# A mixture-of-experts layer on one core: 39 tiles of 256 rows become 25 of 256 and 21 of 128, and the inner columns are cut into chunks of 128

## The chip, the cores and the metric

The kernel runs on one core of a Trainium2 chip. A core has a matrix engine (TensorE, PE in the profile; its weight loads are listed as PEld), a vector engine (DVE), a scalar engine (ACT), a general engine (POOL), an engine that mostly issues transfers (SyncE, SP; SPq are its issues) and 16 DMA engines. Each engine runs its own instructions in order and waits for others by semaphores. The metric is the time of one execution on the device, in microseconds (us).

## What is computed

A transformer block in float32: attention with a residual, then a mixture of experts with a residual. Layernorm stands before and after each half.

```python
x = x + layernorm(attention(layernorm(x)))     # x: (4, 1024, 256), 16 heads of 16, rotary positions
x = x + layernorm(moe(layernorm(x)))

def moe(x):                                     # T = 4096 tokens, D = 256, E = 8 experts, H = 684, K = 2
    d2 = sum(x * x) + sum(cen * cen) - 2 * x @ cen.T
    w, sel = top_k(sqrt(max(d2, 1e-12)), K)     # two experts for each token
    w = softmax(w)
    we = zeros(T, E); we[t, sel] += w
    out = 0
    for e in range(E):
        h = silu(x @ Wg[e] + bg[e]) * (x @ W1[e] + b1[e])    # (T, 684)
        out = out + we[:, e:e + 1] * (h @ W2[e] + b2[e])
    return out
```

The biases bg, b1 and b2 are drawn at random, not zero.

## The kernel before

**Attention.** It takes the first 60% of the span. Its work is cut into steps: a step handles 128 keys against 512 queries for four heads, with scores on TensorE (L671, L678: tiles sc), exp on ACT, the weighted sum on TensorE (L740: av), and for the maxima of steps to come another set of score matmuls (L590: pm) that DVE reduces (L594: part). Between them come works of other kinds: splitting and stacking of heads (L531: ps), values, the output projection (`finish`), layernorm and routing (`settle`). A planner written into the kernel orders all this. A `Work` is a generator that yields before each piece the costs it expects ("P500 D400" means 500 ns of TensorE, then 400 of DVE); works are sorted by due step, and the planner runs the first whose costs fit into the model it keeps of when each engine will be free. The model knows nothing of transfers. TensorE, DVE and ACT execute in the order that the planner emits.

`late_constants` (L191) is such a work, with due step 40: the squares of the centroids, their sum, and the output bias turned through the output projection (pbo, L209). It is issued as soon as it fits.

**Transfers at the start, on SP in program order.** Loads of x and of the attention weights; the wg load of expert 0; then `rows<-empty` (L226), which clears the DRAM tile `rows` (34816 rows: each expert has a region of 4096, since any routing must fit, and 2048 lie behind them) in 34 DMAs of 1 MB; then the building of `wall` (L233 to L248), a DRAM tile that holds for each expert one block of 128 partitions: gate weights, inner weights, output weights in six chunks of 114 rows, and the biases. Per expert these are four DMAs (wg and w1: 128 x 2 x 684, w2: 114 x 6 x 256, b2: one row), and two at the end for bg and b1, all from DRAM to DRAM. Each DMA on SP takes one of eight semaphore lanes in turn, and its issue waits until the DMA that used the lane before has landed; so at most eight are under way.

**Routing.** `settle` finds for each token its two experts and the place in their regions, and scatters the normalized token with its weight and target id to `rows` (L929, on POOL, eight scatters for each 512 tokens). The number of rows per expert is known only at run time.

**Experts.** After attention a small table on DVE (L1038 to L1069) gives each of MT = 39 tiles its expert and its first row: 8192 rows in tiles of 256 are 32, and 7 more cover the incomplete last tiles of the experts, whatever the routing. For each tile j:

- `fetch` (L1076): SP reads the two table entries, loads 256 rows (xt) and the block of the expert's weights (w, a 128-partition part, a 114-partition part and one row; L1085, L1089). Weights are loaded anew for each tile, three buffers deep.
- `transposed` (L1095): four transposes on TensorE (px), one copy on DVE (xT).
- `up` (L1106): for each of six chunks of 114 inner columns four matmuls of 256 columns (two halves of the 256 input channels, gate and inner), Silu on ACT (sil), bias and product on DVE (h).
- `down` (L1127): for each half of the tile's rows six matmuls over the chunks (pe), the 115th row of the last chunk being a row of ones against b2; then the token's weight on DVE (yo) and a scatter on POOL (L1146).

The loop (L1189 on) is written out by hand for SP, TensorE, DVE and ACT: two chunks of up of tile j, half of down of tile j-1, two chunks, the other half, fetch of tile j+2, transposes of tile j+1, two chunks. Then the results of each token's two rows are added, normalized and stored.

A float32 matmul leaves two records in the trace ("x32" is sixteen matmuls).

Of the kernel before, what the change touches and what calls it, by code (L numbers as in the profile page):

```python
# [8 lines left out]
F32 = mybir.dt.float32  # L9
# [7 lines left out]
P = 128  # L17
# [14 lines left out]

TS = 256
NTS = TS // P
MT = 2 * B * T // TS + NE - 1
XW = C + 2
CAP = B * T
NROW = NE * CAP + NE * TS
NRES = 2 * B * T + MT * TS
O1, O2, OG, WW = KC * FF, 2 * KC * FF, 2 * KC * FF + NF * C, 2 * KC * FF + NF * C + 2 * NF  # L40
# [3 lines left out]
def sandwich(  # L44
# [168 lines left out]


# [18 lines left out]
    wall = tc.dram_tile([NE, P, WW], F32, name="wall")  # L233
    for e in range(NE):
        for i, w in enumerate((wg, w1)):
            nc.sync.dma_start(
                out=wall[e, :, i * O1 : (i + 1) * O1].rearrange("p (k f) -> p k f", k=KC),
                in_=w[e].rearrange("(k p) f -> p k f", p=P),
            )
        nc.sync.dma_start(  # L240
            out=wall[e, :FP, O2:OG].rearrange("p (f c) -> p f c", f=NF),
            in_=w2[e].rearrange("(f p) c -> p f c", p=FP),
        )
        nc.sync.dma_start(out=wall[e, FP : FP + 1, OG - C : OG], in_=b2[e : e + 1, :])
    for i, bias in enumerate((bg, b1)):
        nc.sync.dma_start(
            out=wall[:, :FP, OG + i * NF : OG + (i + 1) * NF].rearrange("e p f -> p e f"), in_=bias
        )  # L248
# [353 lines left out]
    def outputs(u, av):  # L602
# [32 lines left out]
        if g == NG - 1:  # L635
            fast = u == len(order) - 1

            before_ = list(settling.values())
            closing[b, qb] = Work(
                finish(b, qb, fast), at_step[0] + 6,  # L640
                after=[back] + [closing[k] for k in closing] + before_[:-1],
            )
            settling[b, qb] = Work(
                settle(b, qb, fast), at_step[0] + 8, after=[closing[b, qb]] + before_
            )
# [346 lines left out]
    with tc.manual_schedule(engines={ET.PE, ET.DVE, ET.Activation}):  # L992
# [17 lines left out]
        Work(late_constants(), 40)  # L1010
# [26 lines left out]

    pc = bank("counts")  # L1038
    nc.tensor.matmul(pc[:, :NE], ones, seen, start=True, stop=True)
    one = slice(0, 1)  # L1040
    cnt = const.tile([1, NE], I32, tag="cnt", name="cnt")
    nc.vector.tensor_scalar(cnt, pc[one, :NE], float(TS - 1), None, ALU.add)
    nc.vector.tensor_scalar(cnt, cnt, TS.bit_length() - 1, None, ALU.arith_shift_right)
    num = const.tile([1, NE], F32, tag="num", name="num")
    nc.vector.tensor_copy(num, cnt)
    tri = const.tile([1, NE, NE], F32, tag="tri", name="tri")
    nc.vector.tensor_tensor(
        tri, num[:, None, :].to_broadcast([1, NE, NE]), before[one], ALU.mult
    )
    first = const.tile([1, NE], F32, tag="first", name="first")  # L1050
    nc.vector.tensor_reduce(first, tri, AX.X, ALU.add)
    sh = [1, MT, NE]
    le = const.tile(sh, F32, tag="le", name="le")
    nc.vector.tensor_tensor(
        le, first[:, None, :].to_broadcast(sh), tiles_at[one, :MT, None].to_broadcast(sh), ALU.is_le
    )
    tab = const.tile([1, 2, MT], F32, tag="tab", name="tab")
    nc.vector.tensor_reduce(tab[:, 0, :], le, AX.X, ALU.add)
    nc.vector.tensor_scalar(tab[:, 0, :], tab[:, 0, :], -1.0, None, ALU.add)
    nc.vector.tensor_tensor(le, le, first[:, None, :].to_broadcast(sh), ALU.mult)  # L1060
    at0 = const.tile([1, MT], F32, tag="at0", name="at0")
    nc.vector.tensor_reduce(at0, le, AX.X, ALU.max)
    nc.vector.tensor_tensor(at0, tiles_at[one, :MT], at0, ALU.subtract)
    nc.vector.tensor_scalar(at0, at0, float(TS), None, ALU.mult)
    nc.vector.scalar_tensor_tensor(
        tab[:, 1, :], tab[:, 0, :], float(CAP), at0, ALU.mult, ALU.add
    )
    tabi = const.tile([1, 2, MT], I32, tag="tabi", name="tabi")
# [3 lines left out]
    hs = [hp.tile([P, NF, TS], F32, tag=f"h{i}", name=f"h{i}") for i in range(2)]  # L1072
    for h in hs:
        nc.gpsimd.memset(h[96:P, NF - 1, :], 1.0)

    def fetch(j):  # L1076
        e = nc.sync.value_load(tabi[:, 0, j : j + 1], min_val=0, max_val=NE - 1)
        r = nc.sync.value_load(tabi[:, 1, j : j + 1], min_val=0, max_val=NROW - TS)
        xt = mp.tile([P, NTS, XW], F32, tag="xt", name=f"xt_{j}")
        nc.sync.dma_start(  # L1080
            out=xt, in_=rows[bass.ds(r, TS), :].rearrange("(i p) c -> p i c", p=P)
        )
        w = wpool.tile([P, WW], F32, tag="w", name=f"w_{j}")
        for rows_, cols in ((P, slice(0, O2)), (FP, slice(O2, WW))):
            nc.sync.dma_start(  # L1085
                out=w[:rows_, cols],
                in_=wall[bass.ds(e, 1), :rows_, cols].rearrange("e p w -> (e p) w"),
            )
        nc.sync.dma_start(  # L1089
            out=w[FP : FP + 1, OG - C : OG],  # L1090
            in_=wall[bass.ds(e, 1), FP : FP + 1, OG - C : OG].rearrange("e p w -> (e p) w"),
        )
        return xt, w

    def transposed(j, xt):  # L1095
        pt = bank(f"px_{j}").rearrange("p (k t) -> p k t", k=KC)
        for i in range(NTS):
            for k in range(KC):
                nc.tensor.transpose(  # L1099
                    pt[:, k, i * P : (i + 1) * P], xt[:, i, k * P : (k + 1) * P], ident  # L1100
                )
        xT = mp.tile([P, KC, TS], F32, tag="xT", name=f"xT_{j}")
        nc.vector.tensor_copy(xT, pt)
        return xT

    def up(j, w, xT, f2):  # L1106

        h = hs[j % 2]
        for f in (2 * f2, 2 * f2 + 1):
            pu = psu.tile([P, 2, TS], F32, tag="pu", name=f"pu_{j}_{f}")  # L1110
            for i in range(2):
                for k in range(KC):
                    c0 = i * O1 + k * FF + f * FP
                    nc.tensor.matmul(  # L1114
                        pu[:FP, i, :], w[:, c0 : c0 + FP], xT[:, k, :],
                        start=(k == 0), stop=(k == KC - 1),
                    )
            sil = sp.tile([FP, TS], F32, tag="sil", name=f"sil_{j}_{f}")
            nc.scalar.activation(  # L1119
                sil, pu[:FP, 0, :], AF.Silu, bias=w[:FP, OG + f : OG + f + 1]  # L1120
            )
            nc.vector.scalar_tensor_tensor(  # L1122
                h[:FP, f, :], pu[:FP, 1, :], w[:FP, OG + NF + f : OG + NF + f + 1], sil,
                ALU.add, ALU.mult,
            )

    def down(j, xt, w, i):  # L1127

        h = hs[j % 2]
        po = bank(f"pe_{j}_{i}")  # L1130
        for f in range(NF):
            n = FP + (f == NF - 1)
            nc.tensor.matmul(  # L1133
                po[:, :C], h[:n, f, i * P : (i + 1) * P], w[:n, O2 + f * C : O2 + (f + 1) * C],
                start=(f == 0), stop=(f == NF - 1),
            )
        y = mp.tile([P, C], F32, tag=f"y{i}", name=f"yo_{j}_{i}")
        ids = mp.tile([P, 1], I32, tag=f"ids{i}", name=f"ids_{j}_{i}")
        own = sp.tile([P, 1], F32, tag=f"own{i}", name=f"own_{j}_{i}")
        at = xt[:, i, C + 1 : C + 2]  # L1140
        nc.vector.tensor_scalar(
            own, at, float(2 * B * T), float(j * TS), ALU.is_ge, ALU.mult
        )
        nc.vector.tensor_tensor(ids, own, at, ALU.add)
        nc.vector.tensor_scalar(y, po[:, :C], xt[:, i, C : C + 1], None, ALU.mult)  # L1145
        sent = nc.gpsimd.indirect_dma_start(  # L1146
            out=res[:, :],
            out_offset=bass.IndirectOffsetOnAxis(ap=ids, axis=0),
            in_=y,
            in_offset=None,  # L1150
        )
        tc.declare_no_dep(sent.ins, group="results", reason="rows of their own")
        tc.add_to_no_dep_group("results", sent.ins)
# [37 lines left out]
    with tc.manual_schedule(engines={ET.SP, ET.PE, ET.DVE, ET.Activation}):  # L1191
        ready, last = [fetch(0), fetch(1)], None
        xT = transposed(0, ready[0][0])
        for j in range(MT):
            xt, w = ready.pop(0)
            up(j, w, xT, 0)
            for i in range(2):
                if last is not None:
                    down(*last, i)
                if i == 1:  # L1200
                    if j + 2 < MT:
                        ready.append(fetch(j + 2))
                    if j + 1 < MT:
                        nxt = transposed(j + 1, ready[0][0])
                up(j, w, xT, i + 1)
            xT, last = nxt, (j, xt, w)
        for i in range(2):
            down(*last, i)
# [86 lines left out]
```

## Time and profile before

| | |
|---|---|
| Time, median of three runs | 1920.45 us (1914.9 to 1924.0) |
| The profiled execution | 1901.81 us, its span 1900.0 us |
| Mean granted TensorE clock | 0.946 |
| TensorE busy | 1699.6 us (89%) |
| DVE, ACT, POOL busy | 1067.6, 880.6, 572.7 us |
| up: matmuls (L1114), ACT (L1119), DVE (L1122) | 422.3, 110.3, 112.9 us busy |
| down: matmuls (L1133) | 214.9 us busy |
| DMA | 101036 packets, 196.99 MB |

The page shows the span in 40 equal slices of 47.5 us; each digit is the busy share of a slice in tenths. "x1872" in a group is its number of records. The granted clock of TensorE by slice is

```profile
PEclk8899999999999999999999995799999999999975
```

and the issues of the transfers that the change touches are listed with their number, size and, for some, the median time from issue to landing:

```profile
w<-wall SPq DMA_DIRECT2D x39, 1368.0 KB, 6.7
rows<-empty SPq DMA_DIRECT2D x34, 1032.0 KB, 15.5
...
wall<-in_w_dram SPq DMA_DIRECT2D x16, 684.0 KB
xt<-rows SPq DMA_DIRECT2D x39, 258.0 KB
wall<-in_wg_dram SPq DMA_DIRECT2D x8, 684.0 KB
```

### The profile page before, as it was taken

The page shows a single profiled execution, that of the slowest core. Times are in us where ns is not written, and L with a number is a line of the kernel's source. Part 1 is how long each engine was busy: PE and PEld are TensorE (multiplying, and loading weights), DVE is VectorE, ACT ScalarE, POOL GpSimd, SP SyncE. Part 2 cuts the span into 40 slices and gives each one's busy share as a digit, 9 for nine tenths or more (in the row PEclk, how much of TensorE's full clock was granted, in tenths as well). Part 3 has the DMA queues.
Part 4 walks back from the last instruction along what each step waited for, and adds up shares of the span by engine and source line. Part 5 has one row for each costly group of instructions (what it writes and reads, how often), then busy time and mean ns, then how long its engine had stood idle before and what let it go on. Part 6 is the DMA issues. An engine that isn't in the chain of part 4 may idle for free. (4 is left out here: it accounts for less than half of the span.)

```text
span 1900.0 us, 27442 instructions
## 1 busy us (share of the span) xinstructions
PE 1699.6 (89%) x9640; PEld 1068.7 (56%) x9640; DVE 1067.6 (56%) x2522; ACT 880.6 (46%) x1766; POOL 572.7 (30%) x1068
## 2 busy tenths in 40 slices
PE   4989999999999999999999992799999999999940
PEld 3444445544444454445444441688888888888840
DVE  6576687686677687676678844133333333333346
ACT  2357676776776676676575671111111111111113
POOL 5652422543471544542432132011111111111104
PEclk8899999999999999999999995799999999999975
DMA  8997500100000001000000001844444444444434
GB/s 251 301 299 207 142 1 12 34 34 12 23 1 23 24 34 34 1 12 23 1 35 18 29 31 36 274 167 163 165 162 163 163 164 167 163 164 166 167 125 155
DMA packets 101036, 196.99 MB, mean 104 GB/s; under 512 B 8094, under 2 KB 80437, under 8 KB 95907
## 3 DMA queue, kind: packets, MB, share of 16 engines
q1 hardware_dynamic: 83410, 160.65, 26.1%
q0 software_dynamic: 9040, 26.21, 4.1%
q10 hardware_dynamic: 8448, 8.39, 1.4%
q8 instruction: 76, 1.25, 0.3%
q14 instruction: 62, 0.50, 0.1%
HBM read 132.22 MB, written 79.86 MB: 112 GB/s over the span
## 5 line engine op out<-in xcount | busy, mean ns | idle before, releaser
L594 DVE TENSOR_REDUCE part<-pm 128x1 f32<-128x512 f32 x1024 | 647.6, 684 | 212.3 <-PE pm L590 209.2
L682 ACT ACTIVATE e<-sc 128x512 f32<-128x512 f32 x1024 | 538.2, 603 | 199.1 <-PE sc L678 191.4
L1114 PE MATMUL pu<-xT,w 128*114 128x256 f32 x1872 | 422.3, 383 | 7.4 <-DMA x<-resid 4.6
L1114 PEld LDWEIGHTS pu<-xT,w 128*114 128x114 f32 x1872 | 334.1, 180 | 77.1 <-issue 5.0
L1119 ACT ACTIVATE sil<-pu,w 114x256 f32<-114x256 f32 x234 | 110.3, 474 | 504.3 <-PE pu L1114 495.4
L1122 DVE SCALAR_TENSOR_TENSOR h<-pu,w,sil 114x256 f32<-114x256 f32 x234 | 112.9, 484 | 337.1 <-ACT sil L1119 337.0
L590 PE MATMUL pm<-stack,stack 64*128 64x512 f32 x960 | 267.9, 472 | 20.3 <-DVE part L594 15.5
L740 PE MATMUL av<-e,v 128*32 128x512 f32 x2048 | 281.7, 622 | 0.0
L1146 POOL DMA_INDIRECT res<-yo,ids x78 | 74.8, 959 | 567.8 <-DVE yo L1145 562.7
L671 PE MATMUL sc<-stack,stack 64*128 64x512 f32 x960 | 238.9, 439 | 1.3 <-ACT oT L766 0.7
L678 PE MATMUL sc<-shift,bring 64*128 64x512 f32 x1024 | 235.3, 407 | 3.7 <-ACT shift L579 3.5
L590 PEld LDWEIGHTS pm<-stack,stack 64*128 64x128 f32 x960 | 120.0, 188 | 200.8 <-DVE part L594 118.2
L1133 PE MATMUL pe<-w,h 114*128 114x256 f32 x936 | 214.9, 379 | 0.0
L1133 PEld LDWEIGHTS pe<-w,h 114*128 114x128 f32 x936 | 178.1, 190 | 25.1
L671 PEld LDWEIGHTS sc<-stack,stack 64*128 64x128 f32 x960 | 114.9, 187 | 64.1 <-issue 23.2
L678 PEld LDWEIGHTS sc<-shift,bring 64*128 64x128 f32 x1024 | 120.6, 190 | 25.8 <-ACT shift L579 14.2
L1145 DVE TENSOR_SCALAR yo<-pe,xt 128x256 f32<-128x256 f32 x78 | 37.7, 483 | 104.4 <-PE pe L1133 104.4
L538 ACT CAST stack<-ps 128x512 fp32r<-128x512 f32 x124 | 73.5, 595 | 49.3 <-PE ps L531 48.9
L531 PEld LDWEIGHTS ps<-ident_r,split 128*128 128x128 f32 x512 | 52.2, 144 | 64.3 <-POOL split L262 22.0
L531 PE MATMUL ps<-ident_r,split 128*128 128x128 f32 x512 | 69.4, 264 | 16.0 <-POOL split L262 15.9
L740 PEld LDWEIGHTS av<-e,v 128*32 128x32 f32 x2048 | 41.2, 109 | 72.6 <-issue 66.3
L929 POOL DMA_INDIRECT rows<-xr,to x64 | 62.7, 980 | 62.3 <-DVE to L924 44.7
(246 smaller groups left out, 1432.6 us busy)
## 6 DMA issues: line engine op xcount, KB each, us to landing
w<-wall SPq DMA_DIRECT2D x39, 1368.0 KB, 6.7
rows<-empty SPq DMA_DIRECT2D x34, 1032.0 KB, 15.5
w<-wall SPq DMA_DIRECT2D x39, 689.3 KB
wall<-in_w_dram SPq DMA_DIRECT2D x16, 684.0 KB
xt<-rows SPq DMA_DIRECT2D x39, 258.0 KB
wall<-in_wg_dram SPq DMA_DIRECT2D x8, 684.0 KB
xb<-in_x_dram POOLq DMA_DIRECT2D x8, 512.0 KB, 4.3
resid<-xb SPq DMA_DIRECT2D x8, 512.0 KB, 3.8
```

Of the source, the lines that this page charges most:

```text
L531: nc.tensor.transpose(ps[:, t * P : (t + 1) * P], splits[b, g, half][:, t, is_k, 2 * pr : 2 * pr + 2].rearrange("p h n d -> p (h n d)"), i ...
L590: nc.tensor.matmul(pm, q[r, t * P : (t + 1) * P], k_[r, half * TB : (half + 1) * TB], start=True, stop=True,)
L594: nc.vector.tensor_reduce(part[:, i, 2 * pr + s, half : half + 1], pm, AX.X, ALU.max)
L671: nc.tensor.matmul(sc, k_[r, kb * P : (kb + 1) * P], q[r, qb * TB : (qb + 1) * TB], start=True, stop=False,)
L678: nc.tensor.matmul(scs[s], bring[pr][r, :], shift[u][r, :], start=False, stop=True)
L682: nc.scalar.activation(e, scs[s], AF.Exp, scale=1.0 / HD**0.5)
L740: nc.tensor.matmul(av[32 * j : 32 * j + 32, :], v_aug[kb][:, 4 * g + j, :], es[j], start=(kb == 0), stop=(kb == NT - 1),)
L1114: nc.tensor.matmul(pu[:FP, i, :], w[:, c0 : c0 + FP], xT[:, k, :], start=(k == 0), stop=(k == KC - 1),)
L1119: nc.scalar.activation(sil, pu[:FP, 0, :], AF.Silu, bias=w[:FP, OG + f : OG + f + 1])
L1122: nc.vector.scalar_tensor_tensor(h[:FP, f, :], pu[:FP, 1, :], w[:FP, OG + NF + f : OG + NF + f + 1], sil, ALU.add, ALU.mult,)
L1133: nc.tensor.matmul(po[:, :C], h[:n, f, i * P : (i + 1) * P], w[:n, O2 + f * C : O2 + (f + 1) * C], start=(f == 0), stop=(f == NF - 1),)
L1146: sent = nc.gpsimd.indirect_dma_start(out=res[:, :], out_offset=bass.IndirectOffsetOnAxis(ap=ids, axis=0), in_=y, in_offset=None,)
```

## The change

**Tiles.** MW = 25 tiles of 256 rows come first: any routing of 8192 rows to eight experts fills at least 25. What each expert has left goes into MH = 21 tiles of 128 rows. 25 x 256 + 21 x 128 = 9088 rows are computed in place of 9984. The table on DVE is made in two parts (`whole_tiles` and `table`, 36 operations for 14). `rows` gets one more clearing DMA (35).

**Chunks.** 684 = 5 x 128 + 44. A chunk of 128 has four matmuls as before. In the remainder, gate and inner share one matmul for each half of the channels: its stationary operand is 44 gate columns followed by the last 64 inner columns, of which w1's last 44 land on partitions 64 to 107. For that wall holds w1's last 64 columns a second time, next to wg. The remainder's h goes to a tile hr: rows 0 to 43 for the tile's first 128 rows, 64 to 107 for the second, each followed by a row of ones for b2. Down issues the remainder's matmuls of both halves first (45 rows each, on different rows of the array), then five chunks for each half.

**Wall and fetch.** Wall is built by eleven DMAs for each expert, 88 in all: wg in two of 128 x 684, w1's last 64 columns in two, its first 640 in two, w2 in one of 128 x 5 x 256, its last 44 rows twice, b2 twice. A fetch is xt, one DMA of 128 x 4068 for all but the remainder of w2, and one of 45 x 256 for each half.

**Biases.** They no longer lie in the layout that wall wants. bg and b1 are loaded to SBUF (`natural`, 114 x 48 each; the load of bg is issued before the clearing of rows, that of b1 after it, by the order in which the tile framework places them on SP); TensorE transposes them (plin), ACT copies them (flat), SP writes them to a DRAM tile (lin) and reads that back as 16 x 684 (lined); TensorE transposes six pieces (pbias_), POOL and ACT fill a tile (biases), and SP writes it to wall. All of this from plin on is in two new pieces of `late_constants`, and `closing`, the work that ends a block of attention, must now come after them.

**Loop.** For each tile: remainder, chunks 0 and 1, first half of down of the tile before, chunks 2 and 3, the rest of down, fetch of j+2, transposes of j+1, chunk 4.

```diff
-MT = 2 * B * T // TS + NE - 1
+MW = -(-(2 * B * T - NE * (TS - 1)) // TS)
+MH = (2 * B * T - MW * TS) // P + NE - 1
+MT = MW + MH
...
@@ late_constants
+        yield "P200 A400"
+        pc = bank("plin", pssc)
+        n = NE * NF
+        for i in range(2):
+            nc.tensor.transpose(pc[:n, i * FP : (i + 1) * FP], natural[:, i, :], ident[:FP, :FP])
+        flat = ap1.tile([n, 2, FP], F32, tag="eq", name="flat")
+        nc.scalar.copy(flat, pc[:n, : 2 * FP].rearrange("p (i f) -> p i f", i=2))
+        for i in range(2):
+            nc.sync.dma_start(
+                out=lin[i].rearrange("e (f p) -> (e f) p", p=FP), in_=flat[:, i, :]
+            )
+        lined = ap1.tile([2 * NE, FF], F32, tag="oT", name="lined")
+        nc.sync.dma_start(out=lined, in_=lin.rearrange("i e f -> (i e) f"))
+        yield "P900 A400"
+        pc = bank("pbias_", pssc).rearrange("p (f i) -> p f i", i=2 * NE)
+        for f in range(NC + 1):
+            m = P if f < NC else FR
+            nc.tensor.transpose(
+                pc[:m, f, :], lined[:, f * P : f * P + m], ident[: 2 * NE, : 2 * NE]
+            )
+        biases = ap1.tile([P, NE, 2, NC + 1], F32, tag="gt", name="biases")
+        pool.memset(biases, 0.0)
...
+        nc.sync.dma_start(
+            out=wall[:, :, OB:OR].rearrange("e p w -> e p w"),
+            in_=biases.rearrange("p e i f -> p e (i f)"),
+        )
...
     wall = tc.dram_tile([NE, P, WW], F32, name="wall")
+    lin = tc.dram_tile([2, NE, FF], F32, name="lin")
+    natural = ap1.tile([FP, 2, NE * NF], F32, tag="gt", name="natural")
+    for i, bias in enumerate((bg, b1)):
+        nc.sync.dma_start(out=natural[:, i, :], in_=bias.rearrange("p e f -> p (e f)"))
     for e in range(NE):
-        for i, w in enumerate((wg, w1)):
-            nc.sync.dma_start(
-                out=wall[e, :, i * O1 : (i + 1) * O1].rearrange("p (k f) -> p k f", k=KC),
-                in_=w[e].rearrange("(k p) f -> p k f", p=P),
-            )
+        for w, to, cols in (
+            (wg, 0, slice(0, FF)), (w1, FF, slice(FF - (P - R2), FF)), (w1, FF + P - R2, slice(0, NC * P))
+        ):
+            n = cols.stop - cols.start
+            for k in range(KC):
+                nc.sync.dma_start(
+                    out=wall[e, :, k * WK + to : k * WK + to + n], in_=w[e, k * P : (k + 1) * P, cols]
+                )
         nc.sync.dma_start(
-            out=wall[e, :FP, O2:OG].rearrange("p (f c) -> p f c", f=NF),
-            in_=w2[e].rearrange("(f p) c -> p f c", p=FP),
-        )
-        nc.sync.dma_start(out=wall[e, FP : FP + 1, OG - C : OG], in_=b2[e : e + 1, :])
+            out=wall[e, :, O2:OB].rearrange("p (f c) -> p f c", f=NC),
+            in_=w2[e, : NC * P].rearrange("(f p) c -> p f c", p=P),
+        )
+        for r in (0, R2):
+            nc.sync.dma_start(out=wall[e, r : r + FR, OR:], in_=w2[e, NC * P :])
+            nc.sync.dma_start(out=wall[e, r + FR : r + FR + 1, OR:], in_=b2[e : e + 1, :])
...
-                after=[back] + [closing[k] for k in closing] + before_[:-1],
+                after=[back, late] + [closing[k] for k in closing] + before_[:-1],
...
-        Work(late_constants(), 40)
+        late = Work(late_constants(), 40)
...
-    def up(j, w, xT, f2):
-
+    def up(j, w, xT, f):
+        n = tiles[j] * P
         h = hs[j % 2]
...
+        pu = psu.tile([P, 2, TS], F32, tag="pu", name=f"pu_{j}_{f}")
+        m = P if f < NC else R2 + FR
+        for i in range(2 if f < NC else 1):
+            for k in range(KC):
+                c0 = k * WK + (i * (FF + P - R2) + f * P)
+                nc.tensor.matmul(
+                    pu[:m, i, :n], w[:, c0 : c0 + m], xT[:, k, :n],
+                    start=(k == 0), stop=(k == KC - 1),
+                )
...
+    def down(j, xt, w):
+
+        pos = [bank(f"pe_{j}_{i}") for i in range(tiles[j])]
+        for i, po in enumerate(pos):
+            r = slice(i * R2, i * R2 + FR + 1)
+            nc.tensor.matmul(po[:, :C], hr[j % 2][r, :], w[r, OR:], start=True, stop=False)
+        for i, po in enumerate(pos):
+            for f in range(NC):
+                nc.tensor.matmul(
+                    po[:, :C], hs[j % 2][:, f, i * P : (i + 1) * P],
+                    w[:, O2 + f * C : O2 + (f + 1) * C], start=False, stop=(f == NC - 1),
+                )
...
-            up(j, w, xT, 0)
...
+            for f in (NC, 0, 1):
+                up(j, w, xT, f)
+            next(last, None)
+            for f in (2, 3):
+                up(j, w, xT, f)
+            for _ in last:
+                pass
+            if j + 2 < MT:
+                ready.append(fetch(j + 2))
+            if j + 1 < MT:
+                nxt = transposed(j + 1, ready[0][0])
+            up(j, w, xT, 4)
+            xT, last = nxt, down(j, xt, w)
+        for _ in last:
+            pass
```

## The prediction

> **What bounds the kernel now.** I read the page first (busy shares and slices), then the chain of waits, then SP's and TensorE's timelines where the diff touches them.
>
> ```profile
> PE 1699.6 (89%) x9640; PEld 1068.7 (56%) x9640; DVE 1067.6 (56%) x2522; ACT 880.6 (46%) x1766; POOL 572.7 (30%) x1068
> PE   4989999999999999999999992799999999999940
> DMA  8997500100000001000000001844444444444434
> ```
>
> TensorE is busy 89% of the span, in tenths 9 through attention (slices 3 to 24) and again in the experts (27 to 37). Whatever TensorE loses in either stage goes to the end, and whatever matrix work falls away in the experts comes off. DMA is loaded in slices 1 to 5, then idle to slice 25.
>
> The chain of waits (start, us, what) in the experts:
>
> ```profile
> 1244.82 6.91 PE pu L1114 x32
> 1251.73 2.59 PE pe L1133 x12
> 1254.32 3.46 PE pu L1114 x16
> 1260.81 6.91 PE pu L1114 x32
> ```
>
> Nothing but TensorE stands there, with a period of 1260.81 - 1244.82 = 15.99 us. One matmul of 256 columns leaves two records, and a record is 6.91/32 = 0.216 us. A tile of 256 rows has 48 records of up (10.37), 24 of down (5.18) and four transposes (0.44 together, from 1260.21 to 1260.65): 15.99. So 39 tiles take 623.4 us.
>
> SP's timeline at the start (start, us, what):
>
> ```profile
> 15.72 0.76 SPq L236 DMA_DIRECT2D wall<-in_wg_dram  x1
> 16.60 117.78 SPq L226 DMA_DIRECT2D rows<-empty  x34
> 134.43 3.37 SPq L236 DMA_DIRECT2D wall<-in_w_dram  x1
> ...
> 145.26 0.83 SPq L236 DMA_DIRECT2D wall<-in_wg_dram  x1
> ...
> 147.86 8.07 SPq L244 DMA_DIRECT2D wall<-in_b_dram  x1
> 155.98 0.64 SPq L236 DMA_DIRECT2D wall<-in_wg_dram  x1
> ```
>
> SP clears the rows for 118 us (3.46 per DMA), then builds wall at 11 us per expert until 228 us. No engine waits for any of it in attention now. TensorE's timeline at that time:
>
> ```profile
> 90.23 1.13 PE L209 MATMUL pbo<-wo,bvs 128*128 128x256 f32 x4
> 91.29 1.07 PE L740 MATMUL av<-e,v 128*32 128x512 f32 x8
> 92.28 0.53 PE L531 MATMUL ps<-ident_r,split 128*128 128x128 f32 x4
> 92.75 0.50 PE L590 MATMUL pm<-stack,stack 64*128 64x512 f32 x2
> 93.08 0.39 PE L671 MATMUL sc<-stack,stack 64*128 64x512 f32 x2
> ```
>
> These five rows are the place where the new bias transposes go.
>
> **Part 1: the biases (a new wait).** The planner runs the late constants early: pbo is at 90.2 us. In the changed kernel's order, TensorE has after pbo four av, four ps, two pm, then the two plin transposes, which wait for both loads of natural; then sc, ps, pm (about 4 us of work), then six pbias_ transposes, which wait for lined. TensorE runs in order, so behind plin stand all scores, and behind them exp on ACT, the maxima on DVE and the rest. POOL's memset of biases waits for plin too, ahead of its splits.
>
> What do the two waits wait for? SP's order is: natural from bg, 35 DMAs of rows, natural from b1, 88 DMAs of wall, two of lin, lined. So lined comes after everything.
> Rows: the last one was issued one step before 134.43; one more DMA (+3.5), one wg load less ahead (a 128x2x684 load moves 256 packets of 2736 B over 16 engines, at 115 ns each in the trace 1.84). The last packets of the rows, at 138.9 to 144.8 by engine, then end near 146.5, and b1 lands at about 148.
> Wall: before, one expert's 11 us are 2 x 1.84 for wg and w1, some 6.5 for w2, whose 114 rows keep only 0.40 of the engines busy (133 GB/s from 166 to 168 us, against 1.04 and 357 GB/s from 162 to 164), and 0.2 per DMA. After: wg 1.84, w1 with the copied block 1.9, w2 of 128 rows 640 packets of 1024 B at 51 ns over 16 engines 2.04, the remainders 0.4: 6.2 us, and 11 DMAs at 0.2 come to 8.4 if nothing overlaps, 6.2 if all does. SP's own issues (0.6 to 0.8 for the large ones, 0.24 for the one-row load at L1089) come to 11 x 0.55 = 6.1. I take 7.7, near the upper one because at most eight DMAs are under way at a time: 62 us for eight experts. A second way: sixteen wo loads of 16 KB took 11.78 us, 0.74 each; 88 x 0.74 = 65. Bounds: 17.4 MB at the best rate of the trace (461 GB/s, 1192 to 1194 us) is 38; the old 11 us is 88.
> Then lin and lined, each issued after the one before has landed, at some 2 us each (a 512 KB store of resid lands after 3.8, of which its 32 packets per engine at 51 ns are 1.6). Lined: 146.5 + 62 + 4 = 212.5.
> TensorE reaches plin at 93.1 and has 4 us of work until lined; it restarts cold (granted clock 0.50 at 1214 to 1216 after an idle time, 1.00 later), 1.5 us once. Lost: 212.5 - 93.1 - 4 + 1.5 = 117, less some 2 that it makes up because DVE is ahead afterwards (all its waits for DVE's sums at L594 to 1150 us are 18 us): **+115, bounds 91 and 141**. The matmuls themselves (8 of at most 128 columns) are under 1 us, ACT's and POOL's copies lie in the idle time. Wall's new end, about 215 instead of 230 us, is a thousand us before its first reader: nothing. Behind lined on SP stand wall's biases and then the first store of resid, which came at 342 us: not reached.
>
> The Trainium skill, "DMA: Bandwidth & Descriptors", "Rules for kernel authors", says that many small transfers should be merged, since under 64 KB one pays mostly overhead; its section on the anatomy of a DMA gives that overhead as about 2 us. It speaks against 88 small DMAs and the detour of lin. Paid one after the other that would be an estimated 176 us for wall, and the time would be some 115 us above mine; the row of sixteen loads at 0.74 shows them overlapping, so I keep the row.
>
> **Part 2: tiles of 256 rows, chunks of 128.** Up goes from 24 to 22 matmuls, down from 12 to 10 and the remainder's pair, which sits on different rows of the array. 44 + 20 records at 0.216 = 13.82, transposes 0.44, the pair 0.43 if its two matmuls run together, 0.86 if not: 14.69 or 15.12. Two score matmuls on 64 rows each took 0.23 us together (806.64 to 806.87 us), so I take 14.69.
>
> **Part 3: tiles of 128 rows.** 44 records of up with 128 columns. No up row of this width exists; the transposes are the nearest: 0.109 per load of 128 columns and its 128-column matmul. The pdist group (96 loads, 11.6 us busy) gives 0.121 as the other end. 44 x 0.109 = 4.80, 12 records of down 2.59, two transposes 0.22: 7.61. Per chunk TensorE takes 0.87 us, ACT and DVE less than their 0.47 and 0.48 at 256 columns: covered. The copy of xT (0.69 at 512 columns) comes late behind DVE's chunk: 0.3. I take 7.9.
> TensorE's page, "TensorE: Matmul & The Clock Gate", "Back-to-back issue gap", gives 81 ns per sustained load and matmul of 128 columns. By it a tile would take an estimated 6.4 us and the 21 tiles 31 us less; the trace's transposes, packed without a gap, show 109, and they decide.
> DMA: a tile needs w of 2.08 MB in its large DMA, 0.05, 0.13 for xt and 0.13 for the scatter: 2.39 MB in 7.9 us is 303 GB/s. Windows with w alone show 384 (1232 to 1234 us), 6.2 us: hidden, with 1.7 us to spare. With a poor rate of 289 (1214 to 1216 us) it is 8.3, and with the issue's delay some 9.0: the upper bound.
> Sum: 25 x 14.69 + 21 x 7.9 = 533, **saved 90**; bounds 96 (7.61 each) and 56 (15.12 and 9.0).
>
> **Part 4: the rest.** The table takes 36 DVE operations for 14 (0.15 to 0.47 us each); it now follows the last settle instead of interleaving with it, and lies under the eight row scatters on POOL (1175.0 to 1185): its cover is some 2 us longer than it; without cover it would be 4. The settle's chain gets shorter: -1 (0 to -3). Fetch issues one large DMA for two and one or two small ones for one, on SP, which is otherwise idle. Closing's extra condition is long met: 0.
>
> **Sum**, on the profiled execution (1901.8, span 1900.0): 1901.8 + 115 - 90 - 1 = 1925.8. The runs' median is 18.6 above the profiled one, so the time I predict is **1944 us**, 1.2% slower. A measurement here can't tell less than about 0.5% (9.6 us) from no change.
>
> **Rivals.**
> A. Lined lands early. The bias loads don't queue behind wall's packets, and SP alone limits: 8 x (7 x 0.45 + 4 x 0.24) = 33 us after b1's issue at 141, and 5 for lin and lined: 179. The stall is 84 and the time 1913, not slower. For it: the xt issue is only 0.40. Against it: SP's b2 issues wait 6 to 10 us each now, so DMAs already hold it up. It decides from lined before 197 us (no loss), 178 for a gain.
> B. Wall still takes 11 us per expert, through overhead of 88 DMAs and eight in flight. For it: 0.74 x 88 is already above my 62. Stall 141, time 1970.
> C. The 128-row tiles are bound by their fetch of 2.39 MB at 9.0 us: 21 x 1.1 = 23 more, with the pair serial 11 more: 1967 to 1978. Against it: the 384 GB/s.
> D. TensorE doesn't stall, the loads being served in time: 1901.8 - 91 + 18.6 = 1829. The order of SP and TensorE speaks against it.
>
> **Chances.** Forecast 0.52 (own range 1928 to 1962), A 0.18, B 0.13, C 0.12, D 0.05. Faster: D and most of the half of A where lined lands by 178, 0.15. Same: the rest of A and the lower edge of the forecast, 0.17. Slower: 0.68. The range reaches from A at 1911 to past B and C at 1984; bounds of both kinds together (91 with 96, 141 with 56) would be 1911 and 2006, and I leave the upper corner and D outside.
>
> **What would show it.** TensorE's slices 3 and 4 at a few tenths, a wait of plin on natural of about 54 us, one of pbias_ on lined of 58, wall's build at 7.7 us per expert, tiles at 14.7 and 7.9 us, waits of up for w below 0.5 us. I am wrong if TensorE is at 9 tenths throughout attention, if lined lands before 197 us, or if the period of the 128-row tiles is set by w.

## The result, and the profile after

The changed kernel takes 1982.8 us (median of four runs, 1980.5 to 1986.2), the kernel before 1920.0: 1.0329 times as long, 95% interval 1.0306 to 1.0352. It is slower by 63 us where I had forecast 24. The profiled execution took 1980.5 us.

The page of the changed kernel, with the rows that answer to those of before:

```profile
PE 1630.3 (82%) x9702; PEld 1014.5 (51%) x9702; DVE 1076.6 (54%) x2597; ACT 889.5 (45%) x1811; POOL 568.0 (29%) x1064
PE   4700499999899999999999999926999999999950
PEclk8855799999999999999999999958999999999985
DMA  9998300001001001000000000017445444577754
```

TensorE works 69 us less (1630.3 for 1699.6), yet the span is 79 us longer: slices 3 and 4 are empty at half the clock, slice 5 is half empty. The last slices of the experts, the tiles of 128 rows, now have a DMA share of 7 tenths.

TensorE's waits in attention (line waited for, us in total, times, longest):

```profile
PE pbias__951 L244 <- DMA lined<-lin: 73.1, 1, 73.1
PE plin L231 <- DMA natural<-in_b_dram: 52.8, 1, 52.8
```

These are the two waits of the prediction, 125.9 us together. SP's timeline shows what lined waits for, here one expert of wall and the end of the list:

```profile
194.46 1.23 SPq L290 DMA_DIRECT2D wall<-in_wg_dram  x2
195.73 4.76 SPq L290 DMA_DIRECT2D wall<-in_w_dram  x4
...
204.05 1.23 SPq L290 DMA_DIRECT2D wall<-in_wg_dram  x2
...
213.28 0.98 SPq L235 DMA_DIRECT2D lin<-flat  x2
217.88 0.30 SPq L239 DMA_DIRECT2D lined<-lin  x1
```

An expert takes 9.6 us in the steady part, the eight of them 78 us (134.9 to 213.3) where I had 62. The row of four issues at 195.73 hides a wait: its issues take 0.5 to 0.6 us each, and the rest of the 4.76 is SP standing still. SP's waits from 130 to 240 us (line waited for, us in total, times, longest) have it as

```profile
SPq L290 <- DMA wall<-in_w_dram: 14.2, 7, 2.7
```

Once per expert the semaphore lane that SP needs next is still held by w2's DMA, issued eight DMAs earlier. In the steady part that is 1.9 to 2.7 us, 2.3 on average, and SP's eleven issues are the other 7.3 us of the 9.6.

In the experts, the chain of waits over one tile of 256 rows (start, us, what):

```profile
1407.35 6.05 PE pu L1202 x28
1413.39 0.63 PE pe L1229 x4
1414.02 2.35 PE pe L1232 x10
1416.38 3.45 PE pu L1202 x16
1419.83 2.16 PE pe L1232 x10
1421.99 0.44 PE px L1185 x4
1422.43 6.05 PE pu L1202 x28
```

The period is 15.08 us, not 14.69. L1229 is the remainder's pair: 0.63 us, and the ten records behind it take 2.35 where the same ten take 2.16 further down: together 0.82 where I had 0.43. Over one tile of 128 rows:

```profile
1762.03 2.44 PE pu L1202 x20
1764.47 0.63 PE pe L1229 x2
1765.10 2.35 PE pe L1232 x10
1767.45 1.78 PE pu L1202 x16
1769.24 0.22 PE px L1185 x2
1769.45 0.89 PE pu L1202 x8
1770.35 0.11 issue
1770.46 2.44 PE pu L1202 x20
```

The period is 8.43 us, not 7.9, and no wait for w stands in it. A record of 128 columns takes 1.78/16 = 0.111. The remainder costs the same 0.63 + 0.19 here, though it is a single matmul (two records).

Between the stages, DVE, POOL and SP:

```profile
1328.88 0.96 POOL L980 DMA_INDIRECT rows<-xr,to  x1 [0.31 <-issue]
1331.86 0.15 DVE L1137 COPY count<-counts 1x8 f32<-1x8 f32 x1 [12.25 <-DMA rows<-xr,to]
...
1340.70 0.41 SPq L1167 DMA_DIRECT2D xt<-rows  x1
```

The table doesn't lie under the scatters, as I had it; its first operation waits 12.25 us, for the last of them to land.

### The profile page after: what moved, and what is told of

It reads as the page before. It is cut to its first block, busy times and chain, and to the rows that moved or that the text cites. A ratio compares the mean times of both kernels' runs of the same rounds, so it can differ in the third digit from the quotient of the medians.

```text
span 1978.7 us, 27856 instructions
## 1 busy us (share of the span) xinstructions
PE 1630.3 (82%) x9702; PEld 1014.5 (51%) x9702; DVE 1076.6 (54%) x2597; ACT 889.5 (45%) x1811; POOL 568.0 (29%) x1064
## 5 line engine op out<-in xcount | busy, mean ns | idle before, releaser
L1202 PE MATMUL pu<-xT,w 128*128 128x256 f32 (+3 forms) x2024 | 361.0, 333 | 7.4 <-DMA w<-wall 5.4
L1202 PEld LDWEIGHTS pu<-xT,w 128*128 128x128 f32 (+1 forms) x2024 | 315.5, 190 | 41.2 <-issue 9.5
L1208 ACT ACTIVATE sil<-pu,w 128x256 f32<-128x256 f32 (+3 forms) x276 | 117.3, 425 | 435.0 <-PE pu L1202 412.4
L1213 DVE SCALAR_TENSOR_TENSOR h<-pu,w,sil 128x256 f32<-128x256 f32 (+1 forms) x230 | 97.3, 423 | 229.7 <-ACT sil L1208 227.3
L1245 POOL DMA_INDIRECT res<-yo,ids x71 | 68.3, 962 | 508.5 <-DVE yo L1244 508.5
L1232 PE MATMUL pe<-w,h 128*128 128x256 f32 x710 | 169.6, 386 | 0.0
L1232 PEld LDWEIGHTS pe<-w,h 128*128 128x128 f32 x710 | 131.0, 190 | 31.2 <-issue 15.3
L1244 DVE TENSOR_SCALAR yo<-pe,xt 128x256 f32<-128x256 f32 x71 | 34.3, 484 | 108.4 <-PE pe L1232 108.4
L582 PE MATMUL ps<-ident_r,split 128*128 128x128 f32 x512 | 70.7, 268 | 16.0 <-POOL split L313 15.9
```

The lines of the kernel that those rows point to most:

```text
L582: nc.tensor.transpose(ps[:, t * P : (t + 1) * P], splits[b, g, half][:, t, is_k, 2 * pr : 2 * pr + 2].rearrange("p h n d -> p (h n d)"), i ...
L1202: nc.tensor.matmul(pu[:m, i, :n], w[:, c0 : c0 + m], xT[:, k, :n], start=(k == 0), stop=(k == KC - 1),)
L1208: nc.scalar.activation(sil[:m, :n], pu[:m, 0, :n], AF.Silu, bias=w[:m, OB + f : OB + f + 1])
L1213: nc.vector.scalar_tensor_tensor(h[:, f, :n], pu[:, 1, :n], bias, sil[:, :n], ALU.add, ALU.mult)
L1232: nc.tensor.matmul(po[:, :C], hs[j % 2][:, f, i * P : (i + 1) * P], w[:, O2 + f * C : O2 + (f + 1) * C], start=False, stop=(f == NC - 1),)
```

## The experiments

The runs fell on two chips. On one the kernel before takes 1920 us, on the other 1893; times are compared within a chip, and ratios are to runs of the kernel before on the same chip.

**The kernel before, a second time.** Its first profiled execution was 18 us under the median of its runs.

> The kernel before, unchanged, for a second profile. Its first profiled execution took 1901.8 us, 18 less than the median of its runs (1920.0); the changed kernel's took 1980.5, 2 less than its median. In the changed kernel's trace the attention steps lose a further 22.7 us behind the two stalls, in single gaps of TensorE of 1 to 3 us that all lie beside the scatters of rows on POOL. Theory: such gaps are in most executions of either kernel and the first profile of before happened to be free of them; then this execution takes 1914 to 1924 us and its trace has several such gaps, 12 to 22 us in sum. Rival: the change causes them; then this one takes about 1902 again, without them.

It took 1918.6 us. The steps of attention start 4.2 us ahead of those of the first profile and end 20.4 behind them; the 24.6 us are lost in single gaps such as this one:

```profile
1058.57 0.39 PE L590 MATMUL pm<-stack,stack 64*128 64x512 f32 x1
...
1060.07 0.96 POOL L929 DMA_INDIRECT rows<-xr,to  x1 [0.30 <-issue]
...
1061.04 1.29 DVE L594 TENSOR_REDUCE part<-pm 128x1 f32<-128x512 f32 x2 [2.96 <-remote]
```

DVE has the sums of 1058.57 before it and starts on them 2 us late, while POOL issues the last scatters; TensorE then waits 2.82 us for DVE. So the gaps aren't the change's, and this profile, not the first, is the one to set beside the changed kernel's (us; each row adds to the one above):

| | first profile of before | second | changed | changed less second |
|---|---|---|---|---|
| attention, to the end of the matmul of the counts | 1168.5 | 1187.3 | 1316.2 | +128.9 |
| from there to the first matmul of up | 28.3 | 28.2 | 36.0 | +7.8 |
| from there to the last scatter of results | 632.6 | 630.6 | 556.6 | -74.0 |
| from there to the end of the span | 70.7 | 70.7 | 69.9 | -0.8 |
| span | 1900.0 | 1916.8 | 1978.7 | +61.9 |

The 61.9 agree with the 62.8 between the medians.

**The biases later.**

```diff
-        late = Work(late_constants(), 40)
+        Work(late_constants(), 40)
+        late = Work(late_biases(), 40, start=34)    # the two new pieces, yield "W25000" between them
```

> The changed kernel with the two bias pieces in a work of their own that may start only at step 34 of attention, with a pause of 25 us in the planner's model between them; SP's order is unchanged. Theory: TensorE reaches plin and pbias_ after their loads have landed, the stall of 126.7 us (lag of the steps behind lined in the trace) goes in full, and the time is 1982.8 - 126 = 1857 us (1848 to 1865), 3.3% under the kernel before. Rival: half of the stall or more comes back somewhere else (SP's stores of resid behind lin, or POOL's memset): over 1890.

1855.5 us, 0.9653 of the kernel before (0.9625 to 0.9681). The whole stall is gone, as the page's slices show, and nothing of it came back:

```profile
PE   4989999989899989899998899259999999999940
```

The experiment leaves every transfer and every matmul of the change in place; only the place of the two bias pieces in the engines' order is different. So the stall of 127 us (1982.8 - 1855.5) is what made the change slower; without it the change gains 64 us.

**Which of the two waits counts.**

```diff
-        nc.sync.dma_start(out=natural[:, i, :], ...)
+        nc.scalar.dma_start(out=natural[:, i, :], ...)
```

> The changed kernel with both loads of natural issued by ACT at its start instead of by SP around the clearing of rows; lin and lined stay behind wall on SP. Theory: only lined's landing sets the end of the stall, so plin's wait of 52.8 us goes, pbias_'s grows from 73 to about 124, and the time stays at 1983 (1975 to 1986). Rival: each of the two waits costs by itself; then 1983 - 53 = 1930.

1978.5 us. plin no longer waits, and the other wait takes it over:

```profile
PE pbias__951 L244 <- DMA lined<-lin: 122.1, 1, 122.1
```

The landing of lined alone sets the end: taking a wait of 52.8 us away gains 4 us.

**The detour itself.** As in the last experiment, with the loads of natural on ACT, and

```diff
-            nc.sync.dma_start(out=lin[i]..., in_=flat[:, i, :])
+            pool.dma_start(out=lin[i]..., in_=flat[:, i, :])
-        nc.sync.dma_start(out=lined, in_=...)
+        pool.dma_start(out=lined, in_=...)
```

> As loads_early, and lin and lined are issued by POOL instead of SP, where TensorE's order is unchanged (plin after pbo, pbias_ some ten instructions later). Theory: what costs is the place behind wall on SP, not the detour itself; three dependent transfers of some 2 to 4 us each leave a wait of 5 to 14 us, and the time is 1857 + 5 to 14 = 1862 to 1871 us. Rival: the detour is slow while rows are being cleared, some 15 us for each transfer (the median from issue to landing of rows<-empty): 1890 to 1905.

1865.8 us, 0.9705 (0.9676 to 0.9735). pbias_ waits 13.7 us for lined in the profiled execution, the slowest of the four. TensorE's order is that of the changed kernel. The three dependent transfers, while the rows are cleared, cost 10 us against late_bias (1865.8 for 1855.5); the other 117 of the 127 us were the place behind the clearing and wall on SP.

**Fewer, larger transfers for wall.**

```diff
-            for k in range(KC):
-                nc.sync.dma_start(out=wall[e, :, k * WK + to : k * WK + to + n], in_=w[e, k * P : (k + 1) * P, cols])
+            nc.sync.dma_start(
+                out=wall[e, :, :O2].rearrange("p (k c) -> p k c", k=KC)[:, :, to : to + n],
+                in_=w[e].rearrange("(k p) f -> p k f", p=P)[:, :, cols],
+            )
```

> The changed kernel with wg and the two pieces of w1 each in one DMA for both channel halves: 8 DMAs per expert for wall in place of 11, the same bytes; the biases stay behind wall as in the change. In the changed kernel's trace the wall takes 9.4 us per expert, where the packets alone would take some 6.2. Theory: SP's issues set this pace (they add up to 9.4 us per expert, with hardly a gap); with three fewer, and none of the waits in the group of four w1 issues, an expert takes some 6.5 to 7.5 us, lined lands 15 to 23 us earlier, and the time is 15 to 23 us less: 1.021 to 1.025 of the kernel before in place of 1.033. Rival: the transfers themselves take 9.4 us; nothing moves, 1.033.

1976.5 us on the chip where the kernel before takes 1894: 1.0441 (1.0415 to 1.0467). Neither held: it is slower than the change's 1.033 (measured on the other chip, where the gaps add about as much to either kernel). SP's timeline of one expert, and SP's waits from 130 to 240 us:

```profile
188.28 0.62 SPq L289 DMA_DIRECT2D wall<-in_wg_dram  x1
188.94 0.62 SPq L293 DMA_DIRECT2D wall<-in_w_dram  x1
195.09 0.57 SPq L289 DMA_DIRECT2D wall<-in_w_dram  x1
...
199.32 0.62 SPq L289 DMA_DIRECT2D wall<-in_wg_dram  x1
```

```profile
SPq L289 <- DMA wall<-in_wg_dram: 45.8, 8, 8.2
```

An expert takes 11.0 us with eight DMAs, 9.6 with eleven. SP stands still for 5.5 us ahead of the DMA at 195.09, a piece of w1. It doesn't wait for a semaphore lane: it waits for the wg of the same expert, issued at 188.28, to land, eight times in all, 5.1 to 6.1 us each in the steady part. The changed kernel has no such wait. The merged DMAs write interleaved columns of the same rows of wall; that the framework takes this for an overlap and orders them is the likely reason, and wasn't tested. The theory had taken SP's rows of the changed kernel for issues alone, where a quarter is waiting. SP's issues fell from 7.3 to 5.6 us per expert, but a new wait of 5.4 replaced one of 2.3. So the experiment doesn't tell what fewer and larger transfers are worth where nothing orders them. The eight experts take 13 us more than in the changed kernel; lined lands 18 us later, since wall also began 5 us later, behind the clearing of the rows, which the edit doesn't touch.

The packets of wall come to 62 us of all 16 engines' time in the changed kernel (7.8 per expert; those of 2736 bytes took 164 ns on average), at a DMA share of 0.80 to 0.87; here they come to 59 at a share of 0.55 to 0.68. In both, the engines run partly empty while SP waits for a landing.

**The table.**

```diff
-        n = hp.tile([1, NE], F32, tag=f"n_{name}", ...)
+        n = const.tile([1, NE], F32, tag=f"n_{name}", ...)    # and the table's other tiles
```

> late_bias with the table's tiles in the pool that lives through the whole kernel instead of the one laid over attention's memory. In the changed kernel's trace the table's first operation starts only after the last rows scatter has landed, and the first fetch comes 25.0 us after the matmul of the counts, against 19.3 before. Theory: the table then runs beside the settle chain and under the scatters; its 36 operations in between delay the scatters by some 2 to 4 us; first fetch some 21 us after the counts, 1855.5 - 4 = 1851 us. Rival: the waiting was for something else (the counts, the scatters' landing), and nothing moves: 1855.

1822.5 us, against 1825.6 of late_bias on the same chip. The first fetch comes 18.2 us after the counts instead of 24.4, but the experts' first tile then waits longer at its start, beside the loads of x from resid, and 3 of the 6 us remain. The two ratios (0.9626, 0.9586 to 0.9667, and 0.9654) can't tell 3 us from nothing by themselves; the trace shows where they come from. In the kernel before, the table's tiles lay in the whole kernel's pool too; moving them to the other pool was part of the change, though it isn't among the lines of the diff shown above.

**The remainder on all rows.**

```diff
-            nc.tensor.matmul(po[:, :C], hr[j % 2][r, :], w[r, OR:], start=True, stop=False)
+            nc.tensor.matmul(po[:, :C], hz[j % 2], w[:, OR:], start=True, stop=False)    # 128-row tiles
```

> late_bias, and in the tiles of 128 rows the remainder's down matmul takes all 128 rows (zeros beside the 45) instead of 45, with w fetched in one DMA of 128 x 4324. In the changed kernel's trace the remainder costs 0.63 us and a further 0.19 before the next matmul's record, 0.82, whether it is one matmul (128-row tiles) or two (256-row tiles), where one full matmul costs 0.43. Theory: what costs is the change between a part of the array's rows and all of them, 0.39 us a time; then the period of the 128-row tiles falls from 8.44 to 8.05 and the time by 21 x 0.39 = 8 us to 1847. Rival: a load and matmul of the remainder is slow for another reason (its h comes late from DVE); then period and time stay, 1855.

Two more transfers fill the rows of wall beside the 45 with zeros. 1818.6 us, against 1825.6. TensorE's timeline (L1244 is the remainder):

```profile
1601.73 0.60 PE L1244 MATMUL pe<-w,hz 128*128 128x256 f32 x2
1602.16 2.32 PE L1247 MATMUL pe<-w,h 128*128 128x256 f32 x10
...
1609.77 0.60 PE L1244 MATMUL pe<-w,hz 128*128 128x256 f32 x2
```

The next group starts 0.43 after the remainder, and the period is 8.04 instead of 8.43. A matmul on all 128 rows, most of them zeros, is 0.39 us cheaper here than one on 45.

**The tiles alone.** The kernel before with 25 and 21 tiles and the two-part table; chunks of 114, wall and biases as they were.

```diff
-MT = 2 * B * T // TS + NE - 1
+MW = -(-(2 * B * T - NE * (TS - 1)) // TS)
+MH = (2 * B * T - MW * TS) // P + NE - 1
+MT = MW + MH
...
-                        pu[:FP, i, :], w[:, c0 : c0 + FP], xT[:, k, :],
+                        pu[:FP, i, :n], w[:, c0 : c0 + FP], xT[:, k, :n],
```

> The kernel before with 25 tiles of 256 and 21 of 128 rows, its table in the whole kernel's pool; inner chunks of 114, wall and biases as before. Theory: 256-row tiles keep 15.99 us, 128-row tiles take 48 x 0.111 + 12 x 0.216 + 0.22 + 0.12 = 8.26; 25 x 15.99 + 21 x 8.26 = 573 against 623.4, 2 us more for the table: 1920 - 48 = 1872 us. So the chunks of 128 bring some 22 us of the experts' gain and the split into tiles 48. Rival: the tiles of 128 rows are bound by their fetch (the 114-row part of w moves at 133 to 155 GB/s in the trace of before, some 6 us beside 2 for the rest): 9 us or more each, over 1886.

1892.4 us, against 1892.3 of the kernel before: 1.000 (0.9972 to 1.0027). The rival is right. TensorE in the tiles of 128 rows:

```profile
1619.96 0.44 PE L1136 MATMUL px<-ident,xt 128*128 128x128 f32 x2 [0.85 <-DMA xt<-rows]
1620.23 1.91 PE L1152 MATMUL pu<-xT,w 128*114 128x128 f32 x16
1623.60 1.97 PE L1152 MATMUL pu<-xT,w 128*114 128x128 f32 x16 [1.46 <-DMA w<-wall]
...
1630.89 0.44 PE L1136 MATMUL px<-ident,xt 128*128 128x128 f32 x2 [0.97 <-DMA xt<-rows]
```

From here on the fetch sets a period of 10.5 to 12.5 us in place of 8.3, and so 21 small tiles cost as much as the 14 large ones that they replace. Two windows in the 128-row tiles, this kernel's and then the changed one's (stretch, busy us of each engine, clock, DMA share, GB/s):

```profile
1596.00:1641.00 45.00, 40.11 (x301) 37.56 (x299) 12.15 (x42) 8.92 (x26) 4.54 (x5) 1.00 0.82 238
```

```profile
1760.00:1800.00 40.00, 39.44 (x278) 35.21 (x277) 15.22 (x49) 10.96 (x30) 4.63 (x5) 1.00 0.81 289
```

At the same share of the engines the part of 128 partitions brings in 289 GB/s, the one with w's 114-row part 238. The chunks of 128 are thus not a small second gain beside the tiles; without them the tiles bring nothing. What the chunks bring without the tiles wasn't run.

**Without the scatters.**

```diff
-            for i in range(2):
+            for i in range(2 if blk == NBLK - 1 else 0):
                 sent = nc.gpsimd.indirect_dma_start(
                     out=rows[:, :],
```

> late_bias without the scatters of rows of the first seven blocks of 512 tokens (so those tokens' rows stay empty; res is filled from empty rows beforehand). Theory: the single gaps of TensorE of 1 to 3 us in attention (some 24 us in sum, in four of the five profiles so far) come from those scatters and go with them: 1855 - 24 = 1831 us, gaps of over 1.2 us only where DVE's maxima or POOL's splits are waited for. Rival: they only happen to lie beside the scatters; the gaps and 1855 stay.

1827.0 us, and no gaps; but it ran on the chip where late_bias with its scatters has none either. It tells nothing, and whether the scatters cause the gaps stays open.

**late_bias on the second chip, and the best version.**

> late_bias once more, to stand beside the next two on one chip. In the last set the kernel before took 1892 instead of 1920 us and no kernel's trace had the single gaps beside the scatters, in the set before that all had them. Theory: those gaps belong to the chip, not to a kernel; the difference to the kernel before is then 64 us where both have them or neither has (0.965 at 1920, 0.966 at 1892). Rival: the gaps are a matter of each kernel; the ratio is then off 0.965 by more than 0.005.

1825.6 us, 0.9654: the same ratio as on the other chip.

> late_bias with early_table and full_rows together. In the traces early_table brings the first matmul of the experts 6.7 us forward and loses 3.5 of it at the experts' start, full_rows takes 0.39 us from each of the 21 tiles of 128 rows. Theory: both add up, 3 + 8 = 11 us less than late_bias_again. Rival: the fetch of 2.21 MB binds the start of the experts more when the first tiles begin earlier; then 8 us or less.

1815.9 us, 0.9593 of the kernel before (0.9568 to 0.9618): 9.7 under late_bias, nearly the sum of the two alone (3.1 and 7.0).

And with both, the remainder on all rows in every tile:

```diff
-            nc.tensor.matmul(po[:, :C], hr[j % 2][r, :], w[r, OR:], start=True, stop=False)
+            nc.tensor.matmul(po[:, :C], hz[j % 2][i], w[:, OR:], start=True, stop=False)
```

> As both, and in the tiles of 256 rows too the remainder's two down matmuls take all 128 rows, one after the other; w is fetched in one DMA. Theory: the pair of 45-row matmuls does run side by side, but the two changes of the array's rows cost as much as that saves: 0.82 us against 2 x 0.43 = 0.86; the period of the 256-row tiles becomes 15.12 instead of 15.08 and the time stays within 2 us of both. Rival: the 0.82 is the pair running one after the other with no cost for the change; then the period stays as well, but that of the 128-row tiles in full_rows would not have fallen.

1815.1 us, 0.9592 (0.9569 to 0.9616). The period of the 256-row tiles is 15.11, where the theory had 15.12. The pair did run side by side (0.82 us for the two, as for the single one of the 128-row tiles), and won nothing by it.

## Why the prediction was wrong

The direction, the mechanism of the stall and its place were right: the two waits stand where I had them, the second sets the end, and the rest of the attention isn't touched. Three terms of the sum failed, all to the same side, by 14, 16 and 8 us; the forecast of +24 became +62.

1. "The stall +115": 129 in the end. The term that failed is wall at 7.7 us per expert: 9.6 measured. I had priced SP's eleven issues at 6.1 us (0.55 each) and the packets at 6.2, and added 1.5 for what doesn't overlap with eight DMAs under way. SP's issues alone took 7.3, and the wait for w2's DMA eight issues back came on top with 2.3. The packets took 7.8; 115 ns for those of 2736 bytes was their median in the trace of before, where their mean was 152. The second way, 65 us from the wo loads, was nearer and still short of 78. The excess of 16 us shows as only 7 at the landing of lined (220 for 212.5), for on SP wall began at 134.9, beside the last rows, and not at 146.5; the two steps of lin and lined took 6.5 instead of 4. The rest of the 14 is TensorE's: it came to plin 2.4 us sooner, had 3 us of work and not 4 between the waits, and against the second profile of before it lost some 3 beyond the two waits, where I had counted on nothing in sum.
2. "Saved 90": 74. The tile of 256 rows is 15.08, not 14.69, by the pair alone. I weighed whether its two matmuls run together or not (0.43 or 0.86) and took a row of attention, 0.23 us for a pair on 64 rows each, whose neighbours use 64 rows too. They do run together, and yet the remainder costs 0.82, 0.39 more than on all rows between neighbours on all rows. The trace of before had a row with the right neighbours, a pair between two groups of 128 rows:

```profile
87.36 0.53 PE L531 MATMUL ps<-ident_r,split 128*128 128x128 f32 x4
87.82 0.50 PE L590 MATMUL pm<-stack,stack 64*128 64x512 f32 x2
88.25 0.53 PE L531 MATMUL ps<-ident_r,split 128*128 128x128 f32 x4
```

From its start to the next it takes 0.43, nearly twice the 0.23. The same change of rows stands in the 128-row tiles, where I had allowed nothing for it: 8.43 for 7.9. There the remainder adds 0.39 and the records of up 0.31 (5.11 for 4.80), and of the 0.3 for the copy of xT an idle time of 0.11 is all that is left. The Trainium skill, "TensorEngine Tiling (Array Packing)", "Key Properties", says that a change of tiling mode drains TensorE. The 0.39 us, there and back, fits that; no run here shows what TensorE does in this time. By the periods alone (25 x 15.08 + 21 x 8.43 = 554) the saving would be 69; the ends of the stage bring the rest of the 74.
3. "-1" for the rest: +7. The step that failed is the cover: I had laid the table under the scatters by its place in DVE's order, and not asked what its tiles lie on. In the pool laid over attention's memory they wait for attention's last reader; back in the whole kernel's pool the first fetch came 6 us sooner.

Rival A (lined early) fell: SP's issues alone took 7.3 us per expert where it had 4.1. Its own terms give a stall of 81 us, not 84, and the lowest corner of the bounds is 1914, not 1911; neither matters for the outcome. B was half right, 9.6 us per expert lying between my 7.7 and its 11. C fell for the changed kernel, whose 128-row tiles wait for w once (1.1 us), and is shown for the chunks of 114. My shift of 18.6 us from the profiled execution to the median came out right by luck: I had no reason for it, and the second profile of before has its 18.8 in attention, in the gaps.

The rows from the trace held where the conditions were the same: 0.111 us for a record of 128 columns with nothing else in the way (I took 0.109), where the 81 ns of the Trainium skill's "TensorE: Matmul & The Clock Gate" ("Back-to-back issue gap") don't fit this float32 stream. The time forecast for the kernel without the stall, 1857 us, was measured as 1855.5.

## What to carry to other kernels

An engine that executes in a hand-made order waits for the slowest thing its order names, so a transfer that nobody waited for becomes the bound when one small read is queued behind it: before a wait is added, list what stands ahead of it on the queue that serves it. Ask of a smaller tile whether its weights still arrive in time, and of a matmul on part of the rows whether zeros on all rows are cheaper where its neighbours use all of them. A price taken from a row of the trace holds only where the neighbours are alike. When transfers are merged, look at what the merged ones now wait for. One profile that is apart from the median of its runs is not a basis for sums; take a second.

## What the runs showed of the hardware

On one chip ACT and DVE start some instructions 1 to 3 us late around POOL's indirect scatters, 23 to 29 us in sum over attention; late_bias, profiled on both chips, shows none of it on the other, and the kernel before takes 1893 us there instead of 1920. The first profile of before shows none either, and on which chip it ran isn't known. A pair of 64-row matmuls takes 0.23 us among its like and 0.43 between groups of 128 rows; a 45-row matmul between full ones takes 0.82, a full one in its place 0.43. After the empty stretch TensorE's granted clock was 0.50, until 225 us, 5 us after its work began again, and 1.00 from 227.
